# A convolution kernel: one of six loaded shifts is copied by VectorE instead

## The chip, the cores and the metric

The kernel runs on one core of a Trainium2 chip. The metric is the device time of one execution in microseconds; before the change the median of three runs is 16687.61 us (16677.77 to 16700.49). TensorE (PE) does the matmuls, VectorE (DVE), ScalarE (ACT) and GpSimd (POOL) move and combine data, SyncE (SP) issues most DMAs. Each engine works through its own instructions in order and waits on semaphores for the others.

## The reference

The input is x, float32, 4 images of 512 x 512 x 16. Two layers follow, each added to x:

```python
# layer 0
x = x + _L0_conv_ref(_gn(x), L0_conv_h0, L0_conv_numerators, L0_conv_denumerator)
# layer 1
x = x + _L1_conv_ref(_gn(x), L1_conv_kernel, L1_conv_bias, L1_conv_radius)
```

`_gn` is a group normalization with 8 groups. Layer 0 is a full two-dimensional convolution with a rational filter, written with Fourier transforms:

```python
H_truncated = jnp.fft.rfft2(b, s=(l1, l2)) / jnp.fft.rfft2(a, s=(l1, l2))
h_truncated = jnp.fft.irfft2(H_truncated, s=(l1, l2))
H_full = h0 + jnp.fft.rfft2(h_truncated, s=(2 * l1, 2 * l2))[0]
X = jnp.fft.rfft2(x, s=(2 * l1, 2 * l2), axes=(-3, -2))
Y = jnp.einsum('...hwi,ijhw->...hwj', X, H_full)
y = jnp.fft.irfft2(Y, s=(2 * l1, 2 * l2), axes=(-3, -2))
return y[..., :l1, :l2, :]
```

Layer 1 is a 3 x 3 convolution whose result is normalized, passed through an arccos and gated with tanh. The change concerns layer 0.

## The kernel before

The program has four phases, one after the other: `filter_phase` makes the filter's taps, `forward_phase` transforms the normalized input along one axis, `conv_phase` does the convolution along the other axis frequency row by frequency row, and `last_phase` transforms back and does layer 1. Only `conv_phase` (L696) is touched.

`conv_phase` runs over 513 rows. A row has an input part x and a filter part g, both in DRAM. Along the remaining axis, positions are split in an outer index t and an inner one s, and the product over t is made as a convolution of 8 by 8 blocks. For this the transformed input of a row, the tile `xe`, is held in eight copies, shifted by 16 partitions each: `xe[:, t]` is the transformed input (128 partitions by 1024 float32) moved by 16 t partitions, where what falls off the end comes from `xl`, the same input turned by the constants `late`. Copy 0 is the transformed input itself. The steps of a row n are spread over several passes of `step`:

- `x_part` (L769): eight matmuls of x with `dfs` into PSUM tiles `px`, evicted to `xe[:, 0]`, one half by ACT and the other by DVE. `turn_x` (L754) makes `dfs_n` for a later row, on ACT and then DVE (L766).
- `x_late` (L784): POOL issues the store of `xe[:, 0]` to the DRAM tile `xf_d`, makes `xl` from `xe[:, 0]` with four products `xu` (L798), one product `xl` (L799) and one sum (L800), and issues the store of `xl` to `xf_d` (L791 both).
- `half_shift` (L806): ACT makes copy 4, a move by 64 partitions, in two halves: partitions 64 to 127 of `xe[:, 0]` go to 0 to 63, and partitions 0 to 63 of `xl` go to 64 to 127 (L809).
- `load_xe` (L812): SP loads the other six copies from `xf_d`, in two DMAs of three shifts each: 1 to 3 and 5 to 7. A shift is a window into `xf_d`, which holds the stored input and the stored `xl` one after the other.
- `g_part` (L821): matmuls of g with `dg` into two PSUM tiles `pg` at a time (pool of 3), evicted to `gh`.
- `mix` (L838): the matmuls of `gh` with all eight copies of `xe`, into `pm`, evicted to `yf`.
- `over_q` (L858) and `over_g` (L888): four chains a row of transposes to `pz`, an ACT copy to `zq` and five DVE operations (L874 to L878), two POOL operations (L882, L884), and matmuls into `py`, evicted to `yo`, which POOL's queue stores (L914).

`step` (L922) interleaves these for several rows: while row n is mixed, g of row n + 1 is transformed, row n - 1 goes through `over_q`, row n + 2 through `x_part`, `x_late` and `half_shift`, and row n + 1 through `load_xe`. A step has four parts k of equal kind. A scheduler then fixes each engine's order, so an engine's order need not be that of the Python lines. `evict` sends every third eviction to DVE and the others to ACT. The pools: `xe` has three buffers, `xl` and `xu` one each, `gh` two, `pm` two banks.

For one row the engines' orders in the program are, from the matmuls `px` on: PE px, mix, pg, pz, mix, pg, pz, py, mix, pg, pz, two of the next pg, mix, pg, pz; ACT zq, xe, half copy from `xe`, yf, turn, gh, zq, half copy from `xl`, yf, gh, zq, yo, yf, gh, zq, yf, gh; DVE z chain, xe, dfs_n, gh, chain, gh, chain, gh, chain, gh; POOL two xu, store issue, two xu, xl, xl, store issue, y_d store, zd, z.

## Time and profile before

| | |
|---|---|
| median of 3 runs | 16687.61 us |
| the profiled execution | 16676.9 us |
| its span | 16675.0 us |
| PE, DVE, ACT, POOL busy over the span | 90%, 64%, 54%, 62% |
| granted TensorE clock, mean | 0.97 |
| HBM read and written | 3030.71 MB and 1477.31 MB |

The convolution takes the slices from about 4760 to 13795 us of the span. In it the page's groups for the operations around the change are:

```profile
L798 POOL TENSOR_TENSOR xu<-xe,c_late 128x256 f32<-128x256 f32 x2052 | 1394.3, 705 | 863.7 <-ACT xe L729 842.8
...
L809 ACT COPY xe<-xl 64x1024 f32<-64x1024 f32 x513 | 538.7, 1050 | 1895.8 <-POOL xl L800 1895.8
...
xe<-xf_d SPq DMA_DIRECT2D x1026, 1536.0 KB
g<-g_d SPq DMA_DIRECT2D x511, 1024.0 KB
```

A group reads: line, engine, operation, the tiles written and read, partitions by elements, count; then busy us in total and mean ns of one; then the engine's idle time just before, and what ended most of it. The last two lines are DMA issues: tile written and read, queue, count, KB of each.

### The profile page before, as it was taken

To read this page: it belongs to the slowest core of one execution; us is meant where nothing else is said; L and a number is where in the kernel's file an instruction comes from. 1 tells how busy PE (TensorE), PEld (TensorE's weight loads), DVE (VectorE), ACT (ScalarE), POOL (GpSimd) and SP (SyncE) were. 2 spreads that over 40 slices of the span, in tenths; PEclk is the share of its full clock that TensorE was granted. 3 is DMA by queue.
4 is the path that set the end of the run, shared out by engine and by line. 5 is a ranking of instruction groups with operands and counts; after the bars stand their busy time and mean duration, and the time that the engine had idled before them with its cause. 6 is when DMAs were issued, how large, how long until landed. Compare 5 with 4: busy or idle time off the path is not lost. (4 is left out here: it accounts for less than half of the span.)

```text
span 16675.0 us, 545650 instructions
## 1 busy us (share of the span) xinstructions
PE 15084.4 (90%) x232588; PEld 11256.3 (68%) x232588; DVE 10610.7 (64%) x22299; ACT 9049.8 (54%) x18799; POOL 10372.0 (62%) x10669
## 2 busy tenths in 40 slices
PE   7999999998988898888888898888888888988888
PEld 5555555554557777777777777777777777867777
DVE  8999999993545555555555555555555552357877
ACT  5666666663345555555555555555555551027888
POOL 7777777772346666666666666666666660237766
PEclk7999999999999999999999999999999999989999
DMA  4888788878878888888888888888888886885531
GB/s 134 231 237 236 233 241 234 237 227 259 248 267 323 325 326 317 321 320 318 321 324 324 325 325 321 324 324 321 324 321 321 324 322 230 312 291 164 169 108 70
DMA packets 2914698, 4543.40 MB, mean 272 GB/s; under 512 B 126114, under 2 KB 2094460, under 8 KB 2801422
## 3 DMA queue, kind: packets, MB, share of 16 engines
q1 hardware_dynamic: 2703070, 3836.37, 67.4%
q0 software_dynamic: 172336, 605.00, 9.4%
q10 hardware_dynamic: 36864, 67.13, 1.2%
q8 instruction: 1833, 30.03, 0.7%
q14 instruction: 595, 4.87, 0.1%
HBM read 3030.71 MB, written 1477.31 MB: 270 GB/s over the span
## 5 line engine op out<-in xcount | busy, mean ns | idle before, releaser
L829 PE MATMUL pg<-c_dg,g 64*128 64x128 f32 x32832 | 2837.4, 290 | 357.0 <-ACT gh L729 186.6
L845 PE MATMUL pm<-xe,gh 128*32 128x64 f32 x131328 | 2386.6, 222 | 538.5 <-issue 286.2
L845 PEld LDWEIGHTS pm<-xe,gh 128*32 128x32 f32 x131328 | 2007.6, 110 | 1133.5 <-issue 933.1
L829 PEld LDWEIGHTS pg<-c_dg,g 64*128 64x128 f32 x32832 | 2286.2, 190 | 692.3 <-issue 260.3
L874 DVE TENSOR_TENSOR z<-zq,pz 128x256 f32<-128x256 f32 x2052 | 861.6, 420 | 2667.5 <-ACT zq L873 2597.6
L727 DVE COPY gh<-pg 128x512 f32<-128x512 f32 x2046 | 1409.9, 689 | 1242.8 <-PE pg L829 1237.6
L449 PE MATMUL pt<-ev_in,c_todd 128*128 128x512 f32 x4096 | 1928.0, 609 | 108.6 <-ACT u L337 83.4
L798 POOL TENSOR_TENSOR xu<-xe,c_late 128x256 f32<-128x256 f32 x2052 | 1394.3, 705 | 863.7 <-ACT xe L729 842.8
L506 DVE RECIPROCAL dn<-dn 128x256 f32<-128x256 f32 x1024 | 1718.1, 1718 | 0.0
L729 ACT COPY yf<-pm 128x512 f32<-128x512 f32 x2046 | 1211.0, 592 | 915.4 <-PE pm L845 901.4
L381 POOL TENSOR_TENSOR sp<-m,dn 128x512 f32<-128x512 f32 x1024 | 1302.6, 1273 | 611.8 <-DVE dn L506 527.1
L809 ACT COPY xe<-xl 64x1024 f32<-64x1024 f32 x513 | 538.7, 1050 | 1895.8 <-POOL xl L800 1895.8
L449 PEld LDWEIGHTS pt<-ev_in,c_todd 128*128 128x128 f32 x4096 | 728.6, 190 | 1022.1 <-issue 701.5
L729 ACT COPY gh<-pg 128x512 f32<-128x512 f32 x2058 | 1201.2, 584 | 378.9 <-PE pg L829 376.6
L866 PE MATMUL pz<-c_ident,yf 128*128 128x128 f32 x8208 | 1372.2, 290 | 29.9 <-issue 17.3
L397 PEld LDWEIGHTS pg<-c_dinv,sp 64*128 64x128 f32 x16384 | 1004.2, 196 | 466.2 <-ACT sp L386 211.4
L408 ACT COPY st<-pg 128x256 f32<-128x256 f32 x2048 | 617.6, 391 | 1281.9 <-PE pg L397 1281.9
L800 POOL TENSOR_TENSOR xl<-xl,xu 128x1024 f32<-128x1024 f32 x513 | 1209.7, 2358 | 40.2
L397 PE MATMUL pg<-c_dinv,sp 64*128 64x128 f32 x16384 | 1106.6, 287 | 72.4 <-ACT sp L386 48.3
L882 POOL TENSOR_TENSOR zd<-z 128x512 f32<-128x512 f32 x513 | 653.1, 1273 | 771.7 <-DVE z L874 771.7
L914 POOL DMA_DIRECT2D y_d<-yo x511 | 297.3, 582 | 1332.6 <-ACT yo L729 1306.8
L1280 PE MATMUL pc<-l_band,xn 128*128 128x160 f32 (+2 forms) x6144 | 1072.9, 333 | 52.2 <-DVE e_o L1335 51.9
(211 smaller groups left out, 30943.8 us busy)
## 6 DMA issues: line engine op xcount, KB each, us to landing
xe<-xf_d SPq DMA_DIRECT2D x1026, 1536.0 KB
g<-g_d SPq DMA_DIRECT2D x511, 1024.0 KB
g_d<-st SPq DMA_DIRECT2D x256, 1024.0 KB
ev_in<-g_d SPq DMA_DIRECT2D x1024, 256.0 KB
g_d<-ot SPq DMA_DIRECT2D x1024, 256.0 KB
xf_d<-xe POOLq DMA_DIRECT2D x513, 448.0 KB, 8.3
xf_d<-xl POOLq DMA_DIRECT2D x513, 448.0 KB, 5.5
x_d<-xo SPq DMA_DIRECT2D x128, 1024.0 KB
```

The lines of the kernel that those rows point to most:

```text
L381: nc.gpsimd.tensor_mul(w["sp"], w["m"], bc(w["dn"], 2, [P, 2, 2, P]))
L397: nc.tensor.matmul(pg[u][:, n, k].rearrange("p a x -> p (a x)"), w["sp"][q, k, c, :], dinv[q, 2 * kp + k, c, :], start=(c == 0), stop=(c = ...
L449: nc.tensor.matmul(pt, todd[:, c, kc, hh * P : hh * P + P], ev[:, kc, c], start=(kc == 0), stop=(kc == 1),)
L506: nc.vector.reciprocal(w["dn"], w["dn"])
L727: nc.vector.tensor_copy(dst, src)
L729: nc.scalar.copy(dst, src)
L798: nc.gpsimd.tensor_mul(u[:, :, h, c], xe[:, :, h, 1 - c], bc(late[:, 1 + c], 2, [P, F, 2]))
L800: nc.gpsimd.tensor_add(xl.rearrange("p f h c k -> p (f h c k)"), xl.rearrange("p f h c k -> p (f h c k)"), u.rearrange("p f h c k -> p (f ...
L829: nc.tensor.matmul(pg[c][:, j % 4], g[half, j], dg[half], start=True, stop=True)
L845: nc.tensor.matmul(pm[32 * q : 32 * q + 32, g % 8], gh[:, f].rearrange("p c j -> p (c j)"), xe[:, :, f].rearrange("p t h c k -> p t (h c k ...
L866: nc.tensor.transpose(pz[:, t % 4].rearrange("p v q x -> p (v q x)"), y[:, at].rearrange("p g x -> p (g x)"), ident)
L1280: nc.tensor.matmul(pc[:, lo:hi, :].rearrange("p w j -> p (w j)"), xns[q][:, h * P + dh : h * P + dh + P], bands[dh][:, o : o + hi - lo, :] ...
```

## The change

Copy 2, a move by 32 partitions, is no longer loaded. DVE makes it in four quarters of 32 partitions: three from `xe[:, 0]`, one from `xl`. In the Python order the first three are called in part k = 1 of a step and the last in part k = 3. The first load now brings shifts 1 and 3 (1024 KB), the second still 5 to 7. New and changed code:

```diff
+        def quarter_shift(n, late):
+
+            for q in range(3, 4) if late else range(3):
+                src = state["xl"][:32] if late else state["xe", n][32 * q + 32 : 32 * q + 64, 0]
+                nc.vector.tensor_copy(state["xe", n][32 * q : 32 * q + 32, 2].rearrange("p f h c k -> p (f h c k)"),
+                                      src.rearrange("p f h c k -> p (f h c k)"))
+
         def load_xe(n):
             src = xf_d[n % 4]
-            for t in (1, 5):
+            for t in (slice(1, 4, 2), slice(5, 8)):
+                of = range(8)[t]
                 nc.sync.dma_start(
-                    out=state["xe", n][:, t : t + 3].rearrange("p t f h c k -> p t (f h c k)"),
-                    in_=bass.AP(tensor=src.tensor, offset=src.offset + t * C * XF,
-                                ap=[[XF, P], [C * XF, 3], [1, XF]]),
+                    out=state["xe", n][:, t].rearrange("p t f h c k -> p t (f h c k)"),
+                    in_=bass.AP(tensor=src.tensor, offset=src.offset + of[0] * C * XF,
+                                ap=[[XF, P], [of.step * C * XF, len(of)], [1, XF]]),
                 )
@@ step
                 if row(2) and k >= 2:
                     half_shift(n + 2, k - 2)
+                if row(2) and k % 2:
+                    quarter_shift(n + 2, k == 3)
```

What the scheduler makes of it: in a steady row, DVE's order becomes chain, xe, dfs_n, three quarters from `xe`, gh, the first three operations of the next chain, the quarter from `xl`, the last two operations of that chain, gh, chain, gh, chain, gh. SP's order becomes both loads of xe, g, x, where it was load of xe, g, load of xe, x. The orders of PE, ACT and POOL in a steady row are as before.

## The prediction

> **What bounds the kernel now.** I read the span's slices first, then the convolution's stretch by itself, then its waits, then one row in order of time. The convolution runs from about 4760 to 13795 us, 513 rows (the page counts 513 of L800), so a microsecond per row is worth 513 us. The stretch inside it:

> ```profile
> 4900.00:13800.00 8900.00, 7953.99 (x181488) 6366.20 (x181487) 4844.57 (x13109) 4697.17 (x8570) 5684.39 (x5546) 0.98 0.87 322
> ```

> After the window and its length stand PE, PEld, DVE, ACT and POOL busy, the granted clock, the DMA share and GB/s. PE is busy 89%, the DMA engines 87%, DVE 54%, POOL 64%. Shares alone would say "PE, with DMA close behind". The waits, from 5000 to 13500 us (482 rows), say how close:

> ```profile
> ACT xe L809 <- POOL xl L800: 1782.8, 482, 6.5
> ...
> PEld pg L829 <- ACT gh L729: 220.7, 220, 4.1
> ...
> PE pm L845 <- DMA xe<-xf_d: 110.7, 75, 3.5
> ```

> (us in total, times, longest.) The load of xe, which the change shrinks, stops PE in 75 of 482 rows: 110.7/482 = 0.23 us per row. ACT waits for POOL's xl in every row. One row shows what that wait sets:

> ```profile
> 9097.97 1.89 PE L777 MATMUL px<-dfs_n,x 128*128 128x256 f32 x8
> ...
> 9099.03 0.59 ACT L729 COPY xe<-px 128x512 f32<-128x512 f32 x1 [0.45 <-PE px L777]
> ...
> 9099.70 1.36 POOL L798 TENSOR_TENSOR xu<-xe,c_late 128x256 f32<-128x256 f32 x2 [1.07 <-ACT xe L729]
> ...
> 9100.80 0.54 DVE L766 SCALAR_TENSOR_TENSOR dfs_n<-c_dfs,own,turn 128x256 f32<-128x256 f32 x1
> ...
> 9101.17 0.57 POOL L791 DMA_DIRECT2D xf_d<-xe  x1
> 9101.77 1.37 POOL L798 TENSOR_TENSOR xu<-xe,c_late 128x256 f32<-128x256 f32 x2
> ...
> 9103.09 1.96 POOL L799 TENSOR_TENSOR xl<-xe,c_late 128x1024 f32<-128x1024 f32 x1
> ...
> 9105.13 2.36 POOL L800 TENSOR_TENSOR xl<-xl,xu 128x1024 f32<-128x1024 f32 x1
> ...
> 9107.52 1.04 ACT L809 COPY xe<-xl 64x1024 f32<-64x1024 f32 x1 [3.74 <-POOL xl L800]
> ...
> 9109.97 0.42 DVE L874 TENSOR_TENSOR z<-zq,pz 128x256 f32<-128x256 f32 x1 [3.97 <-ACT zq L873]
> ...
> 9111.48 0.68 DVE L727 COPY gh<-pg 128x512 f32<-128x512 f32 x1
> ...
> 9112.27 1.10 PE L845 MATMUL pm<-xe,gh 128*32 128x64 f32 x64 [0.39 <-DVE gh L727]
> ...
> 9114.88 0.38 PE L777 MATMUL px<-dfs_n,x 128*128 128x256 f32 x1
> ```

> Follow the releases: px (0), ACT's eviction of px, POOL without a gap from 1.73 to 9.52, ACT's late half copy, behind it in ACT's queue yf, gh, zq, then DVE's zq/pz chain (12.00), behind that DVE's last gh (13.51), which the next row's first mix needs (14.30), then px again: 16.91 us. This closes without PE being the limit. Taking px starts from the timeline between 6000 and 13000 us (396 rows), the 5th and 25th percentiles of the row are 16.90 and 16.93, the median 17.17, the mean 17.66: a sharp floor, with a tail from PE's own stalls. The tail's parts: the third pz of a row stands at 12.84 in floor rows and on average 0.54 later; the rest of the row is 0.19 over. So the floor is POOL's path, and only 0.73 us of the mean row is anything else.

> [...] A copy of 128x8 takes 164 and 166 ns, and once 1320, beside a POOL instruction that starts with it:

> ```profile
> 15511.48 1.32 DVE L1092 COPY gn_mu<-mv 128x8 f32<-128x8 f32 x1
> 15511.49 1.28 POOL L1326 TENSOR_TENSOR e_gate<-e_gate,e_y 128x512 f32<-128x512 f32 x1
> ```

> And POOL waits for DVE[...]: the same 128x2048 operation takes 4.52 us alone and 6.44 when DVE's has 2.05 us left:

> ```profile
> 4060.27 2.28 DVE L664 TENSOR_TENSOR xu<-xw 128x2048 f32<-128x2048 f32 x1
> ...
> 4060.50 6.44 POOL L663 TENSOR_TENSOR xt<-xw 128x2048 f32<-128x2048 f32 x1 [13.29 <-DVE xw L660]
> ...
> 4066.89 4.52 POOL L665 TENSOR_TENSOR xt<-xw 128x2048 f32<-128x2048 f32 x1
> ```

> [...]

> **The change part by part.** *Removed:* one of six loaded shifts, 128 partitions x 4 KB = 0.52 MB of 5.69 MB per row (2740.96 MB in 482 rows), 9% of the traffic. At most it ends PE's 0.23 us of DMA waits. The second load also moves ahead of g on SP's queue, so xe lands after 2.6 MB rather than after 4.2; g, used a row later, has room. Both help, and the 0.23 is all there is to help. PE's "issue" gaps I leave alone.

> *Added to DVE:* four copies of 32x1024. Price: [...]0.69 us each[...]. DVE idles 8.1 us a row (17.66 - 9.6), so the 2.8 us fit by amount. Place decides.

> *Early three.* In DVE's order they come right after dfs_n (L766), before gh. That end is at about 3.4 after px: just as POOL has the xf_d<-xe issue (3.20 to 3.77), then two L798 of 0.70, L799 and L800, all on the floor's path. By the exclusion each copy takes a turn against POOL: the first against the issue, the others between the L798s and L799. POOL loses what the copies hold: three times about 0.6 us of the 0.69, **1.8 us**. Bounds: nothing if the copies don't exclude POOL; 3 x 0.69 = 2.1 if all is held[...]. A gain for POOL is excluded: nothing of its queue is removed. I take 1.8, since the traces above show whole waits (1.92 of 2.05).

> DVE's own side of this is covered: the copies end near 7.2, gh at 7.9 instead of 4.8 and its buffer is wanted by PE's third pg, after 11.

> *Late one.* DVE's order puts it inside the first zq/pz chain, after L876. It waits for xl, as ACT's copy does. Behind it stand L877, L878, gh and the second chain. From xl: 0.7 + 0.2 + 0.3 + 0.7 = 1.9 us, while zq releases the second chain 2.5 us after xl (9.52 to 12.00). So it is hidden, by 0.6 us[...]. It holds back POOL's store issue by up to 0.7, but loads have a row of room.

> *Sum per row.* Floor 16.93 + 1.8 = 18.73. A longer floor absorbs late PE: of the 0.54 excess only 0.15 lies beyond 1.8 us (same 396 rows). The rest 0.19 less 0.23 of DMA waits is about nothing. New mean 18.84 against 17.66: +1.18 x 513 = +605 us on the profiled 16676.9 (span 16675.0), 17282; the runs' median is 10.7 above the profiled execution: **17290**.

> The ends: 1.2 us (0.4 a copy) gives 18.32, +339, about 17030; 2.1 gives 19.08, +730, about 17420.

> **The rivals.**
> 1. *The exclusion doesn't reach these copies*[...]. Then floor unchanged, 0.23 us a row gained: 513 x 0.23 = 118, 16570, or 16525 if PE's issue gaps (PE's four "issue" rows in the waits, 463 us in 482 rows) shrink by the 9% of traffic. For it: [...]DVE has idle time. Against: the 1.32 us copy and the 6.44 us POOL instruction. This is the other side; it decides from a POOL delay of about 0.35 us a row downwards: 0.35 plus the 0.42 of PE excess that lies beyond it equals the 0.54 + 0.23 that there is to lose or gain now.
> 2. *POOL keeps its turn and the copies starve* until L800 ends, 9.5. Then copies to 11.6, gh 12.3, chain and late copy to 14, second chain to 16.5, gh 17.2: the mix is 2.9 late, +2.2 a row after absorption, 17820. [...] For it: POOL's next instruction starts before the last ends. Against: the 1.32 us copy waited for one instruction only.
> 3. *Both cancel*, a POOL delay of 0.3 to 0.4 us: the time stays.

> **How the numbers follow.** Forecast 0.67 (its own range 17030 to 17420), rival 1 0.22, rival 2 with slow copies 0.08, rival 3 0.03. A measurement of this kernel can tell about 0.2% (33 us) from no change. Slower 0.67 + 0.08 = 0.75, same 0.03, faster 0.22. The range takes in half of rival 1 and the upper bound of the forecast: 16540 to 17480, leaving out about 0.19.

> **What would show it.** Right: in the changed profile the xf_d<-xe issue, L798 or L799 are longer by what the three copies take, and their sum from px to xl's end is 11.3 us instead of 9.5; the shortest rows grow from 16.9 to about 18.7; waits for xe's DMA go; DMA falls to about 5.16 MB a row, 0.74 busy. The copies' records would be longer than 0.69, with waiting in them. Wrong: POOL's durations unchanged and rows still at 16.9 (rival 1), or DVE's early copies only after L800 (rival 2). A late copy that ends past the second chain's release would add a term that I put at nothing.

## The result, and the profile after

| | before | after |
|---|---|---|
| median | 16682.69 us (16665.89 to 16700.49, 4 runs) | 18692.49 us (18688.12 to 18698.38, 4 runs) |
| span of the profiled execution | 16675.0 us | 18689.8 us |
| granted TensorE clock, mean | 0.970 | 0.891 |
| DVE busy over the span | 64% | 79% |
| HBM read | 3030.71 MB | 2761.76 MB |
| mean row of the convolution | 17.66 us | 21.61 us |

The ratio is 1.1205 [1.1185, 1.1224]: 2010 us slower, where 605 had been forecast. The rows account for it: 3.95 us x 513 = 2026. Rows are measured here as in the prediction, from the start of one px to the next, between 6000 and 13000 us of the span.

The groups of the page after the change show where the engines' own time went (busy us, mean ns, then idle time before and its releaser):

```profile
L816 DVE COPY xe<-xe 32x1024 f32<-32x1024 f32 x1539 | 3906.8, 2539 | 30.9 <-ACT xe L729 0.9
...
L798 POOL TENSOR_TENSOR xu<-xe,c_late 128x256 f32<-128x256 f32 x2052 | 1391.3, 702 | 1767.9 <-ACT xe L729 1748.7
...
L800 POOL TENSOR_TENSOR xl<-xl,xu 128x1024 f32<-128x1024 f32 x513 | 1385.2, 2700 | 40.2
```

An early copy takes 2.54 us on average. The late one, the same operation on the same amount of data, takes 0.686. So three of them hold DVE for 7.6 us in a row, 5.6 of it in waiting (experiments 1 and 2 show that it is waiting), and the page counts this as busy: DVE's 79% is no sign of work. POOL, which was to pay, has L798 unchanged (705 ns before) and L800 longer by 0.34 us (2.36 before).

One row in order of time (start, us, engine, line, then in brackets what ended an idle time before it):

```profile
10009.61 2.50 PE L777 MATMUL px<-dfs_n,x 128*128 128x256 f32 x8
...
10013.63 7.66 DVE L816 COPY xe<-xe 32x1024 f32<-32x1024 f32 x3
10013.86 1.35 POOL L798 TENSOR_TENSOR xu<-xe,c_late 128x256 f32<-128x256 f32 x2
...
10015.18 1.97 POOL L799 TENSOR_TENSOR xl<-xe,c_late 128x1024 f32<-128x1024 f32 x1
...
10017.22 2.70 POOL L800 TENSOR_TENSOR xl<-xl,xu 128x1024 f32<-128x1024 f32 x1
...
10021.32 0.69 DVE L727 COPY gh<-pg 128x512 f32<-128x512 f32 x1
...
10022.07 1.25 PE L837 MATMUL pg<-c_dg,g 64*128 64x128 f32 x16 [1.62 <-DVE gh L727]
...
10023.15 0.69 DVE L816 COPY xe<-xl 32x1024 f32<-32x1024 f32 x1
...
10026.36 0.68 DVE L727 COPY gh<-pg 128x512 f32<-128x512 f32 x1
...
10027.15 1.93 PE L853 MATMUL pm<-xe,gh 128*32 128x64 f32 x64 [0.95 <-issue]
...
10031.64 0.38 PE L777 MATMUL px<-dfs_n,x 128*128 128x256 f32 x1
```

The three copies begin 0.23 us before POOL's second pair of L798, and end 1.4 us after L800. The records of the single copies give 4.06, 2.77 and 0.81 us: the first ends 0.55 us after L799 has ended, so it came in at the boundary to L800, and L800 is the instruction that is 0.34 us longer; the second ends after L800; the third has POOL's queue nearly empty beside it. At the boundaries before (store issue to L798, L798 to L798, L798 to L799) no copy came in. Behind the copies stands gh, at 11.7 us after px in this row, where it stood at 4.1 to 5.5 before. PE's third pg waits 1.62 us for it, the chains and the last gh follow, and the next mix begins 17.54 us after px. In the shortest rows (5th percentile, 6000 to 13000 us) it begins 16.98 us after px, where it was 14.28: 2.7 us later. On average it begins at 17.18, where it was 14.93: 2.25 us of the 3.95.

The rest, 1.70 us, lies between that mix and the next px: 4.43 us on average, where it was 2.73. It is 4.49 in this row and 2.61 in the one shown of before, with the same matmuls in it. The windows of this row say why (after the window and its length: PE, PEld, DVE, ACT, POOL busy, then granted clock, DMA share, GB/s):

```profile
10013.00:10022.00 9.00, 7.45 (x196) 5.72 (x184) 8.91 (x5) 4.74 (x9) 7.41 (x7) 1.00 0.35 108
...
10024.40:10027.10 2.70, 1.79 (x6) 1.17 (x6) 2.60 (x8) 0.37 (x1) 0.00 (x0) 0.52 0.84 282
10027.10:10031.60 4.50, 4.45 (x82) 4.09 (x83) 2.03 (x6) 1.06 (x2) 2.52 (x2) 0.53 1.01 400
```

After PE's waits for gh (1.62 us) and for the z chain (1.09 us) its clock is granted at half (0.52 and 0.53 in the two windows), and the next 64 matmuls of mix take 1.93 us instead of 1.10. From 6000 to 13000 us of the changed kernel 2171 of 7000 us are recorded at half clock; in the kernel before 266. The same windows show DVE busy for nearly all of the time from the copies to the mix: over all rows it is idle for 0.32 us (median) between the start of the first early copy and the end of the gh that the mix waits for. PE's waits from 5000 to 14500 us (us in total, times, longest):

```profile
PE pg L837 <- DVE gh L727: 701.9, 435, 1.8
PE pm L853 <- issue: 526.2, 443, 1.7
PE pz L874 <- DVE z L886: 473.3, 436, 1.1
```

All three stand in nearly each of the 440 rows. Of the second the profile names no cause ("issue"), but the last mix begins 0.10 us after the end of the gh before it, at the 5th percentile of the rows as at the 95th, so it is a wait for DVE too. In the convolution before (5000 to 13500 us) the first did not occur and the third came to 0.4 us in all. The waits for xe's DMA (110.7 us before) are gone.

### The profile page after: what moved, and what is told of

Its sections match the earlier page's. It is cut to its first block, busy times and chain, and to the rows that moved or that the text cites. A ratio compares the mean times of both kernels' runs of the same rounds, so it can differ in the third digit from the quotient of the medians.

```text
span 18689.8 us, 547709 instructions
## 1 busy us (share of the span) xinstructions
PE 16058.1 (86%) x232588; PEld 12126.5 (65%) x232588; DVE 14850.1 (79%) x24351; ACT 9011.6 (48%) x18799; POOL 10630.6 (57%) x10669
## 3 DMA queue, kind: packets, MB, share of 16 engines
HBM read 2761.76 MB, written 1477.31 MB: 227 GB/s over the span
## 5 line engine op out<-in xcount | busy, mean ns | idle before, releaser
L816 DVE COPY xe<-xe 32x1024 f32<-32x1024 f32 x1539 | 3906.8, 2539 | 30.9 <-ACT xe L729 0.9
L837 PE MATMUL pg<-c_dg,g 64*128 64x128 f32 x32832 | 3207.9, 321 | 838.2 <-DVE gh L727 813.5
L837 PEld LDWEIGHTS pg<-c_dg,g 64*128 64x128 f32 x32832 | 2644.9, 218 | 1248.8 <-DVE gh L727 929.4
L853 PE MATMUL pm<-xe,gh 128*32 128x64 f32 x131328 | 2693.4, 244 | 625.5 <-issue 612.4
L853 PEld LDWEIGHTS pm<-xe,gh 128*32 128x32 f32 x131328 | 2333.9, 125 | 1197.2 <-issue 1182.0
L798 POOL TENSOR_TENSOR xu<-xe,c_late 128x256 f32<-128x256 f32 x2052 | 1391.3, 702 | 1767.9 <-ACT xe L729 1748.7
L727 DVE COPY gh<-pg 128x512 f32<-128x512 f32 x2046 | 1406.1, 687 | 1099.7 <-PE pg L837 1083.5
L874 PE MATMUL pz<-c_ident,yf 128*128 128x128 f32 x8208 | 1583.4, 324 | 548.4 <-DVE z L886 548.2
L729 ACT COPY yf<-pm 128x512 f32<-128x512 f32 x2046 | 1215.4, 594 | 1724.1 <-PE pm L853 1711.8
L874 PEld LDWEIGHTS pz<-c_ident,yf 128*128 128x128 f32 x8208 | 1016.5, 160 | 868.2 <-DVE z L886 644.1
L809 ACT COPY xe<-xl 64x1024 f32<-64x1024 f32 x513 | 538.3, 1049 | 2114.4 <-POOL xl L800 2114.4
L729 ACT COPY gh<-pg 128x512 f32<-128x512 f32 x2058 | 1200.2, 583 | 674.1 <-PE pg L837 674.1
L800 POOL TENSOR_TENSOR xl<-xl,xu 128x1024 f32<-128x1024 f32 x513 | 1385.2, 2700 | 40.2
L881 ACT COPY zq<-pz 128x256 f32<-128x256 f32 x2052 | 774.0, 377 | 869.3 <-PE pz L874 584.5
```

What stands on the lines that cost most here:

```text
L727: nc.vector.tensor_copy(dst, src)
L729: nc.scalar.copy(dst, src)
L798: nc.gpsimd.tensor_mul(u[:, :, h, c], xe[:, :, h, 1 - c], bc(late[:, 1 + c], 2, [P, F, 2]))
L800: nc.gpsimd.tensor_add(xl.rearrange("p f h c k -> p (f h c k)"), xl.rearrange("p f h c k -> p (f h c k)"), u.rearrange("p f h c k -> p (f ...
L816: nc.vector.tensor_copy(state["xe", n][32 * q : 32 * q + 32, 2].rearrange("p f h c k -> p (f h c k)"), src.rearrange("p f h c k -> p (f h ...
L837: nc.tensor.matmul(pg[c][:, j % 4], g[half, j], dg[half], start=True, stop=True)
```

## The experiments

Three questions: is it the copies' waiting that costs 2010 us; how much of it is the clock; and why does a smaller load not gain anything. Times are medians; the ratio is to the kernel before, run on the same chip.

**1. The quarters made by a sum in place of the copy.** The same four moves at the same place on DVE, as a sum over an axis of one element, which leaves the values as they are:

```diff
-                nc.vector.tensor_copy(state["xe", n][32 * q : 32 * q + 32, 2].rearrange("p f h c k -> p (f h c k)"),
-                                      src.rearrange("p f h c k -> p (f h c k)"))
+                nc.vector.reduce_sum(state["xe", n][32 * q : 32 * q + 32, 2].rearrange("p f h c k -> p (f h c k)"),
+                                     src.rearrange("p f h c k -> p (f h c k)").unsqueeze(2), axis=AX.X)
```

> All four quarters stay on DVE in the same part of the row, but are made by a tensor_reduce over an axis of one element: [...]. Theory A (the early copies stand still[...]): the waits go although DVE has more work; the L816 group shows about 1.2 us each, rows 17.3 to 17.9 us, total 16500 to 16850, granted clock back at 0.97. Rival B (DVE simply gets too much work in a queue that PE waits for): 4.9 us a row instead of 2.8 is worse than the changed kernel, over 18700. Rival C (the clock of PE, not the waits, makes the loss): the clock must stay low here too, about 18000 or more.

Measured: 16754.69 us, ratio 1.0047 [1.0033, 1.0061]. The groups of its page:

```profile
L816 DVE TENSOR_REDUCE xe<-xe 32x1024 f32<-32x1024 f32 x1539 | 1862.7, 1210 | 39.2
...
L800 POOL TENSOR_TENSOR xl<-xl,xu 128x1024 f32<-128x1024 f32 x513 | 1210.0, 2359 | 40.2
```

An operation that takes almost twice as long by itself (1.21 us against 0.69) removes 96% of the loss. Each of the 1539 takes between 1.206 and 1.217 us whatever POOL does, and L800 is back at 2.36. So neither DVE's load nor the place in its queue was the cost, but the copies' waiting for POOL.

**2. The same copies at another place.** The order of DVE fixed by hand: the late quarter and two early ones behind the gh that follows xl, the last one behind the last gh.

```diff
+        order = InOrder(tc, nc.vector)
...
+                with order if k >= 2 else ExitStack():
+                    if row(1):
+                        for j in range(4):
+                            g_part(n + 1, 4 * k + j)
+                    if row(2) and k >= 2:
+                        quarter_shift(n + 2, (3, 0, 1) if k == 2 else (2,))
+                    if row(-1):
+                        for t in range(4):
+                            over_q(n - 1, 4 * k + t)
```

> [...]DVE's order is fixed so that none runs beside POOL's products: the late one and two early ones after xl is done, between gh and the second zq/pz chain, the fourth after the last gh. Theory A: every copy takes its 0.69 us, none waits for more than POOL's store issue; they end at about 11.7 us after px, just before zq releases the second chain at 12.0; rows 16.9 to 17.9 us, total 16400 to 16850. Rival B (amount of DVE work): as the changed kernel, about 18690. If the prediction's own price were right (POOL loses what the copies hold), the place also cures it; this run doesn't part A from that, the length of L798 to L800 in the changed kernel does (they are as before but for 0.35 us of L800).

Measured: 16803.07 us, ratio 1.0070 [1.0051, 1.0090]. The copies take 0.68 to 0.69 us (5th to 95th percentile), and L800 is at 2.358 us. Away from POOL's run of L798 to L800 the very instructions that cost 12% cost 0.7. With the first experiment this fixes the cause from two sides: this operation, at that place.

**3. The clock.** The changed kernel with more work for PE in the gaps (a third mix, the fourth part of g and the transposes of one part are done twice or three times, with the same results):

```diff
-                        mix(n, 8 * k + g)
+                        mix(n, 8 * k + g, 2 if k == 2 else 1)
...
-                        g_part(n + 1, 4 * k + j)
+                        g_part(n + 1, 4 * k + j, 2 if k == 3 else 1)
...
+            for _ in range(3 if k == 3 else 1):
```

> The changed kernel, with PE given more to do where it waits: in each row the matmuls of the third mix and of the fourth g part are done twice and the transposes of the fourth part three times, with the same results (about 1.1 + 1.2 + 1.3 = 3.6 us of PE work a row at full clock). Theory A+C (after PE's gaps the granted clock falls to half for part of each row, which lengthens the matmuls behind the gaps by about 1.5 us a row): the clock rises from 0.84 in the convolution to over 0.95 and the kernel gets faster although it does more, 17700 to 18200. Rival (the waits alone make the loss and the clock is only a sign of them): no gain, 18690 or more, up to 19500 if the added work is not hidden.

Measured: 18117.52 us, ratio 1.0858 [1.0835, 1.0880], granted clock 0.98 in the convolution against 0.84, and the copies wait as before (4.16, 2.75, 0.81 us). The changed kernel and this one, from 5000 to 13500 us, in the columns given above:

```profile
5000.00:13500.00 8500.00, 6960.64 (x141662) 5639.88 (x141663) 7044.34 (x11798) 3635.74 (x6687) 4639.47 (x4330) 0.84 0.65 239
5000.00:13500.00 8500.00, 7502.48 (x186440) 6210.64 (x186438) 7465.17 (x12494) 3936.24 (x7078) 4874.06 (x4578) 0.98 0.68 254
```

More matmuls, and 575 us less. The shortest rows are 19.61 us, which is the old 16.9 plus the 2.7 by which mix is late there: without the clock's part the floor has moved by exactly the late mix. As the added matmuls take time too, the clock's part of the 2010 us is at least 575. The rows give an upper figure: the stretch from the last mix to px, which was 1.70 us longer in the changed kernel, is back at 2.71 us here, and 1.70 x 513 is 872. So some 575 to 870 us belong to the clock and the other 1140 to 1440 to the waits themselves.

**4. Shorter instructions on POOL.** The changed kernel with L799 and L800 cut into four quarters each, in the order product, sum, product, sum:

```diff
+            for i in range(4):
+                at = slice(i * F // 4, (i + 1) * F // 4)
+                with order:
+                    nc.gpsimd.tensor_mul(xl[:, at].rearrange("p f h c k -> p f (h c k)"), fl[:, at],
+                                         bc(late[:, 0][:, at], 2, [P, F // 4, 8]))
+                    part = xl[:, at].rearrange("p f h c k -> p (f h c k)")
+                    nc.gpsimd.tensor_add(part, part, u[:, at].rearrange("p f h c k -> p (f h c k)"))
```

> The changed kernel, with GpSimd's product L799 and sum L800 each cut into four quarters in the order product, sum, product, sum, so that GpSimd waits for a result of its own four times instead of once; nothing else changes. Theory [...]: the three early copies come in ahead of the first, second and third sum, so the first takes 2.6 to 3.4 us instead of 4.13, the second and third 1.6 to 2.2 each (2.77 and 0.80 before), the sum of the three stays at 6.5 to 7.5, and gh behind them starts at 9.8 to 10.8 after px instead of 11.2; 18000 to 18700 us. Rival (a waiting copy comes in only after GpSimd has run empty): the first copy takes over 7 us, until the last sum is done, and gh starts at 12.5 or later. Rival (the wait belongs to the copy's place on VectorE, not to GpSimd's queue): durations 4.1, 2.8, 0.8 as before.

Measured: 17934.65 us, in one run, so the durations are used here and not the time. A row in order of time (L800 is here the product xu, L804 the product and L807 the sum for xl):

```profile
10026.62 4.48 DVE L821 COPY xe<-xe 32x1024 f32<-32x1024 f32 x3
...
10026.94 1.34 POOL L800 TENSOR_TENSOR xu<-xe,c_late 128x256 f32<-128x256 f32 x2
...
10028.25 1.15 POOL L804 TENSOR_TENSOR xl<-xe,c_late 128x256 f32<-128x256 f32 x1
10029.48 1.06 POOL L807 TENSOR_TENSOR xl<-xl,xu 128x256 f32<-128x256 f32 x1
10030.50 1.08 POOL L804 TENSOR_TENSOR xl<-xe,c_late 128x256 f32<-128x256 f32 x1
10031.13 0.69 DVE L727 COPY gh<-pg 128x512 f32<-128x512 f32 x1
10031.66 0.72 POOL L807 TENSOR_TENSOR xl<-xl,xu 128x256 f32<-128x256 f32 x1
```

The three copies now take 4.48 us instead of 7.66 (2.31, 1.03 and 1.12 at the median), and gh stands at 7.9 us after px instead of 11.2. Each of POOL's first three short instructions is longer by 0.34 to 0.52 us (an undisturbed product takes 0.63, a sum 0.72), so here POOL does pay for the copies. The copies' waiting fell when nothing but POOL's instructions was changed, so POOL's queue sets it. But my rule for it falls: a copy was to come in only where POOL waits for its own last result, and the third came in between a sum and a product that does not use it, the first between the last xu and the first product. Which boundaries let a copy in stays open: in the changed kernel, the boundary from the last xu to the long L799 did not.

**5. The smaller load by itself.** Five shifts are loaded, nothing is copied; the copy shifted by 32 partitions is set to zero by one memset, so that shift's products are left out of the result, with the same matmuls for PE:

```diff
-                if row(2) and k % 2:
-                    quarter_shift(n + 2, k == 3)
+                if row(2) and k == 3:
+                    with order:
+                        nc.vector.memset(state["xe", n + 2][:, 2].rearrange("p f h c k -> p (f h c k)"), 0.0)
```

> The load is made smaller and nothing is copied: five shifts are loaded as in the changed kernel, and the copy shifted by 32 partitions is filled with zeros by one memset on VectorE behind the last gh of the row, so this kernel leaves out the products of that shift. The floor of a row (16.9 us, late half copy ahead of yf and gh on ScalarE) is untouched. Theory 1 (the rows stand above their floor because the DMA engines are 87% busy): with a sixth of the loaded copies gone the mean row falls from 17.66 towards 17.0, and the run takes 16300 to 16450 us. Theory 2 (what stands above the floor is TensorE waiting for blocks of its own instructions, each 16 KB packet of the instruction queue landing some 1.4 us before the gap ends, however much is loaded): the mean row stays at 17.5 to 17.8 and the run at 16600 to 16760 us.

Measured: 16831.72 us, ratio 1.0099 [1.0082, 1.0116]. The DMA engines are 79% busy instead of 87, and the kernel is slower by 172 us, beyond both theories. The floor is where it was (5th percentile 16.88 us); the mean row rose to 17.99. Three rows in four are at 16.9 to 17.7, and one in six takes some 22 (65 of 389 are over 20 us). The timeline of the first experiment, whose rows do the same, shows such a row, with PE stopped in the middle of a mix for nothing that the trace names:

```profile
6216.85 0.97 PE L853 MATMUL pm<-xe,gh 128*32 128x64 f32 x52 [1.57 <-issue]
...
6224.16 0.44 PE L853 MATMUL pm<-xe,gh 128*32 128x64 f32 x8 [3.73 <-issue]
```

What lands just before such stops end can be counted in the DMA records, where packets of 16 KB and 8 KB on two queues are marked "instruction". The number of those of 16 KB goes with that of PE's instructions: 2.83 a row before, with 720 matmuls and weight loads, and 3.52 in experiment 3, with 896; both grew by the factor 1.24. From 6000 to 13000 us, of PE's idle times of more than 1.2 us before a matmul, those that end within 1.6 us after such a packet has landed (the sums of 337, 417 and 457 us in the expectations count such stops a little more widely):

| | gaps | of these behind an instruction packet | their sum |
|---|---|---|---|
| before | 196 | 175 | 315 us |
| quarters by a sum (1) | 249 | 242 | 458 us |
| smaller load alone (5) | 219 | 215 | 440 us |
| changed kernel | 429 | 105 | 177 us |

In the changed kernel the share is 24%, what chance would give at its 1113 packets; its gaps are the waits for DVE. In the others it is 89 to 98%, where chance would give about 30%, and the ends keep a narrow distance from the landing (1.2 to 1.5 us in experiment 5, 5th to 95th percentile). So what stands above the floor of a row is, as far as this coincidence shows, mostly PE waiting for its own instructions. It is 0.80 us a row before (315 us in 395 rows) and 1.13 in experiment 5, and the difference is the 0.33 us by which the mean row rose. The packets before a stop take no longer than the others (0.95 us at the median for both, experiment 5), so what is late is their start. At 2.83 packets a row the boundaries between them come back to the same place in a row's instructions every sixth row (6 x 2.83 = 17.0), and 54 of the 64 distances from one long row to the next are 5 to 7 rows. That fits the beat; why it comes with the smaller load it does not say, since the kernel before has as many packets a row and no such beat.

**6. The floor by itself.** The kernel before, with ACT's late half copy ordered behind zq of part 2:

```diff
+        order = InOrder(tc, nc.scalar)
...
+                    with order if k == 2 else ExitStack():
+                        for t in range(4):
+                            over_q(n - 1, 4 * k + t)
...
+                    with order if k == 3 else ExitStack():
+                        half_shift(n + 2, k - 2)
```

> The kernel before, with one edit: ACT's copy of xl into the second half of shift 4 is ordered behind the zq of part 2, so that yf, gh and zq of that part no longer wait for POOL's xl in ACT's queue. Nothing else changes. If the prediction's reading of the floor is right (POOL's path through ACT's queue sets the shortest row, 16.9 us, and PE isn't the limit there), rows get shorter: PE's own work is about 15.3 us a row, so the floor falls to 15.8 to 16.6 and the total to 16100 to 16500. Rival (PE or the DMA engines set the row): unchanged within 0.3%, 16640 to 16740.

Measured: 16673.59 us, ratio 0.9996 [0.9988, 1.0005]. The prediction's floor is right (the 5th percentile of the row fell from 16.90 to 15.67 us), but the expected gain did not come: the mean row is 17.63 instead of 17.66. The waits from 5000 to 13500 us:

```profile
ACT xe L809 <- POOL xl L800: 528.8, 352, 4.6
PE pm L847 <- issue: 345.9, 324, 3.5
PE pm L847 <- DMA xe<-xf_d: 261.8, 136, 4.4
```

ACT's wait for xl was 1782.8 us before, and PE's two waits 257 and 111. These two have grown by 0.5 us a row, which is a part of what took the gain away.

**7. Both together, on DVE and on ACT.** The quarters by reduce with the order of the sixth experiment; and a version in which ACT copies the early three right behind zq of part 1 and DVE the late one. In the second, the late half copy also comes to stand behind zq of part 2:

```diff
-                nc.vector.tensor_copy(state["xe", n][32 * q : 32 * q + 32, 2].rearrange("p f h c k -> p (f h c k)"),
-                                      src.rearrange("p f h c k -> p (f h c k)"))
+                (nc.vector.tensor_copy if late else nc.scalar.copy)(
+                    state["xe", n][32 * q : 32 * q + 32, 2].rearrange("p f h c k -> p (f h c k)"),
+                    src.rearrange("p f h c k -> p (f h c k)"))
...
+                    with order if k == 1 else ExitStack():
...
+                if row(2) and k == 1:
+                    with order:
+                        quarter_shift(n + 2, False)
+                if row(2) and k == 3:
+                    quarter_shift(n + 2, True)
```

> The quarters by tensor_reduce on VectorE (1.21 us each, no wait for GpSimd) and ScalarE's late half copy ordered behind zq of part 2: smaller load and lower floor (15.7 us) together. Theory 1 (bytes held the mean in the reordered kernel, 5.7 MB a row at 322 GB/s): now 5.2 MB, row 16.0 to 16.5, 16100 to 16400 us. Theory 2 (instruction blocks, with TensorE itself busy 15.3 to 15.7 us of a row): row 17.2 to 17.8, 16450 to 16750 us.

> The three early quarters are copied by ScalarE right behind zq of part 1 (three more instructions on ScalarE, estimated at 1.04 us each from the 64x1024 copies), the late one by VectorE; in the planned order the late half copy now also stands behind yf, gh and zq of part 2, as in the reordered kernel before. [...]nothing of the 2000 us remains: the one late copy takes 0.69 us, L800 2.36 us. Then the two theories of the mean row part: if DMA bytes held it, row 16.0 to 16.5 and 16100 to 16400 us; if TensorE's waits for instruction blocks hold it, row 17.2 to 17.8 and 16450 to 16750 us. If ScalarE is too full with three more copies (9.3 of 16.8 us busy before, 12.4 with them), gh and yf come later and the run is slower than before, 16800 to 17200 us.

Measured: by reduce 16863.46 us, ratio 1.0122 [1.0107, 1.0137], above all that was expected; by ACT 16525.68 us, ratio 0.9921 [0.9906, 0.9935]. The second is 0.8% faster than the kernel before. Its groups:

```profile
L818 ACT COPY xe<-xe 32x1024 f32<-32x1024 f32 x1539 | 1607.2, 1044 | 24.6
...
L800 POOL TENSOR_TENSOR xl<-xl,xu 128x1024 f32<-128x1024 f32 x513 | 1209.4, 2357 | 40.2
...
L818 DVE COPY xe<-xl 32x1024 f32<-32x1024 f32 x513 | 352.2, 686 | 1281.6 <-POOL xl L800 1281.5
```

ACT needs 1.04 us for a copy that DVE makes in 0.69, but none of the 1539 takes more than 1.063. The shortest rows are at 16.1 us, the mean at 17.42; of PE's gaps 207 of 217 end behind an instruction packet, 406 us. With the reduces the floor stayed at 16.8, and the starts in its timeline say through what: the late quarter waits for xl on DVE until 9.47 us after px and takes 1.21, the rest of the first chain and gh stand behind it, and the second chain starts at 11.91, where it started at 12.00 behind ACT's late half copy. The reordering on ACT took away one path from xl and left the other.

**8. The place of g in SP's queue.** In all kernels with five loaded shifts so far g stood behind both loads of xe. Three runs move it: the order of the kernel before (first load, g, second load) for the smaller load alone and for the version on ACT, and, for the latter, the second load behind g and x:

```diff
             with queue:
                 if row(1):
                     load_xe(n + 1, 0)
                 if row(2):
                     load_g(n + 2)
                 if row(1):
                     load_xe(n + 1, 1)
```

> The kernel with the smaller load and zeros for the copy shifted by 32 partitions (it leaves out that shift's products), with SyncE's queue in the order of the kernel before: first xe load, g, second xe load. In the changed kernel and in every kernel with five loaded shifts so far g stood behind both xe loads. Theory (the place of g in the queue is what made the smaller load a loss: TensorE's instruction blocks fall behind 8 us of full DMA engines at the wrong moment): the run comes back from 16832 to 16550 to 16700 us, and TensorE's waits of over 1.2 us that end behind an instruction packet drop from 457 us in 7000 to the 337 of the kernel before or less. Rival (the order of the queue is nothing, the regular beat of rows comes with the smaller load itself): 16800 to 16860 us.

> The kernel with the early quarters on ScalarE, with SyncE's queue in the order of the kernel before: first xe load, g, second xe load. Theory (g's place): mean row falls from 17.42 by 0.2 to 0.6 us, 16200 to 16420 us. Rival (the order is nothing): 16490 to 16560 us.

> The kernel with the early quarters on ScalarE, with the second xe load behind g and x in SyncE's queue, so that it is issued some 4 us later and the DMA engines aren't full for 8 us at a stretch. Theory (TensorE's instruction blocks queue behind the long burst of loads): its waits of over 1.2 us behind an instruction packet fall from 417 us in 7000 to under 300, and the run takes 16150 to 16400 us. Rival (the waits have another cause): 16490 to 16560 us. If the second load lands too late for the next row: 16700 us or more, with TensorE waiting for the load.

Measured: 16845.71 us, ratio 1.0099 [1.0083, 1.0116]; 16538.44 us, 0.9919 [0.9897, 0.9941]; 16604.47 us, 0.9957 [0.9942, 0.9972]. The first two are where they were with g last, and the sums of PE's gaps behind instruction packets too (431 and 386 us; 393 in the third). So for g's place the rival holds. The third lies between the ranges that were expected, some 0.4% slower than with g last, and it does not test what it was made for: the second load was issued 1.5 us after the first (median) instead of 0.42, which is far from the 4 us that were meant, and the stretches with the DMA engines over 90% full are as long as with g last (10.4 us against 10.6). Whether a shorter burst of loads would help, why the instructions come late, and why a smaller load makes the long rows regular, is open.

## Why the prediction was wrong

The direction was right, the size was not: 17290 with a range up to 17480, and 18692 measured.

**Removed: right in the bytes.** 239 GB/s x 21.61 us = 5.16 MB a row, as forecast, and PE's waits for xe's DMA went. That this would gain up to 0.23 us a row was wrong in sign, by itself it came with 0.33 us more (experiment 5).

**The price of a copy: right.** The 0.69 us were my estimate, which no trace of before shows; 0.686 measured where nothing is in its way.

**Early three: the step that failed.** "By the exclusion each copy takes a turn against POOL ... POOL loses what the copies hold: ... 1.8 us." That one engine holds the other up is there, the turns are not: POOL lost 0.34 us, and the copies lost 5.6. The turns were my supposition; no trace of before shows them. I had argued from the 1.32 us copy, which waited for one POOL instruction, and from the 6.44 us POOL instruction, where DVE's instruction had begun 0.23 us earlier. Neither shows a DVE copy that comes upon a queue of POOL instructions with no gap between them, and that was the case here, plain in the very timeline that the prediction shows: store issue, two L798, L799 and L800 each start where the last one ends. And a copy that had been waiting for 1.5 us (from 10013.63) still saw L799 go first (at 10015.18).

**DVE's own side: the cover that was gone.** "The copies end near 7.2, gh at 7.9 ... its buffer is wanted by PE's third pg, after 11" was a sound statement of the slack, 3 us, and the only thing needed to price the other outcome. With the copies ending at 11.16 the slack was overrun: gh from 11.2 to 11.9, a wait of 1.62 us before pg in the row shown, and the last mix 2.7 us late in the shortest rows.

**The late quarter: its price was right, but it was not hidden.** It takes 0.686 us inside the first chain, as priced. It was to end before zq releases the second chain. It ended 13.70 us after px (median), and that release came at 12.24; the second chain began only at 14.73, behind gh. As DVE hardly idles on the way to the mix, the late copy's 0.69 us are part of the 2.7. The prediction had named the sign, "a term that I put at nothing"; the delay of the early three brought it about. In the version on ACT the copy ends at 10.15, the release comes at 10.30, and it is hidden.

**The second rival was the mechanism.** "The copies starve until L800 ends ... the mix is 2.9 late": two of three did, and mix was 2.7 late in the shortest rows. Its tail was to absorb 0.7 us of that; 0.45 was absorbed, as the mix is 2.25 late on average, so its +2.2 a row was close. What it lacked was any term for the clock: 1.70 us a row by the stretch behind the last mix, and 2.25 + 1.70 are the 3.95 measured. Its chance of 0.08 rested on one copy that waited for one instruction.

**Floor and mean.** That POOL's path sets the floor is shown (experiment 6). But "only 0.73 us of the mean row is anything else" does not mean that a shorter path shortens the mean row: with that path shortened by 1.2 us, the mean row stayed at 17.63, as PE's other waits grew.

## What to carry to other kernels

Before you put a copy like this one on VectorE (32x1024 float32 from one SBUF tile to another), look at what GpSimd has queued at that moment: if its instructions follow each other without a gap, price the copy at the length of the whole run, not at one instruction (three copies of 0.69 us took 7.66 us here and ended 1.4 us after GpSimd's run), and price everything behind it on VectorE at that delay. ScalarE (1.04 us a copy here), or a VectorE operation that does not wait for GpSimd (the sum, 1.21 us), can be the cheaper choice though each instruction is slower: ratios of 0.9921 (with ScalarE's order changed too) and 1.0047 here, against 1.1205. And when a new wait stops TensorE in every row, price the clock too: the 64 matmuls after the waits took 1.93 us here instead of 1.10.
